# Row factors of a graph-attention layer fetched from DRAM by SyncE, and the first expert gathers placed later

## The chip, the cores and the metric

The kernel runs on one core of one Trainium2 chip. The metric is device time in microseconds (us) of one execution. Engines are named as in the profile: PE is TensorE (PEld its weight loads), DVE is VectorE, ACT is ScalarE, POOL is GpSimd, SP is SyncE. SP computes nothing here; it issues transfers. POOL issues the gathers and scatters whose rows are given by a list of indices. A queue name such as SPq or POOLq is the instruction stream of that engine.

## The reference, cut to what matters

The input is a matrix x of 3327 rows and 256 columns and a symmetric 0/1 adjacency matrix of 3327 by 3327. Two layers follow each other, each with two residual steps:

```
x = x + L0_gnn(layernorm(x), adj)        # attention over the graph, 2 heads of 128 columns
x = x + L0_ffn(layernorm(x))             # 16 experts, 2 of them for each row
x = x + L1_gnn(layernorm(x), adj)        # attention over the graph, 1 head of 256 columns, elu
x = x + L1_ffn(layernorm(x))             # 30 steps of a recurrence with a 256x256 product
```

The attention of layer 0, for row i, column j and head h:

```
s1, s2 = per row and head, two numbers          # products of the row with fixed vectors
e   = leaky_relu(s1[i] + s2[j], 0.2)
att = softmax over j of e, only where adj[i, j] == 1
out[i] = sum_j att[i, j] * W3h[j]
```

Because the exponential of a leaky relu is the larger of two exponentials, the kernel never computes a 3327 by 3327 exponential. It keeps one factor per row i (`row`) and two or three per column j (`full`, `part`, `minus`), and each weight is `relu(row_i * full_j - part_j) + part_j`, multiplied by the adjacency bit. The softmax's sum comes out of the same product, from a column of ones that stands beside W3h.

The expert step of layer 0 takes for every row the two experts with the largest gate values, and adds the two results with their weights.

## The kernel before, in words

**Tiling.** The rows are in 26 tiles of 128 (NT, the last tile has 127 rows). The attention of a layer is the function `attend` (L201). It works in parts: a part is one group of row tiles and one head. In layer 0 the groups (L45) have 4, 6, 6, 6 and 4 tiles, and each is done for head 0 and then head 1, so there are ten parts; in this text they are numbered 0 to 9. In layer 1 there is one head and the groups have three tiles (the last one has two), which gives nine parts.

**One part.** For each of the 26 column tiles j, three engines take turns. ACT makes `e`, 128 by n*128 numbers, from the row factors `rb` (L276). DVE adds and masks with the adjacency into `pT` (L281). PE multiplies each of the n tiles of `pT` with the features of tile j and accumulates into PSUM (L286); each of these float32 products is two PE instructions. `e` and `pT` have three buffers each. When a part is through, `close` (L252) divides by the sums, and after head 1 it goes on to the group's routing. This is done in small steps during the columns of the next part (L291).

**Row factors.** `rb` holds the row factors of the part's rows, the same on all 128 partitions. There are two such buffers (`rows_p`, L506). In layer 0, `row_factors` (L229) makes them on chip: for every tile of the part PE multiplies the factor column, repeated, with the identity matrix (L243, again two PE instructions for each tile), and ACT copies the result from PSUM into `rb` (L247), at most four tiles in a copy. In layer 1 only the first part does that. There, `put_factors` (L221) turns all factors with one PE transposition, DVE copies them to SBUF, and SP writes them to a DRAM tensor `factors`; the later parts are filled by one SP transfer each that reads the same DRAM rows for all 128 partitions (L234).

**Order.** The code calls `row_factors` for the following part at the middle column of the running part (L273, j = 13). What is executed is set by the framework's planner: it keeps the data dependences, takes the code's order as the priority, and puts an instruction ahead of others on its engine when it expects it to be ready first. A buffer of a pool is given to whoever comes first in that order once it is free. The trace shows such moves: the L243 products of parts 0, 1 and 2 all run from 48.74 us on, before the first attention product. [...]

**The graph.** The adjacency arrives in five pieces, one per group of row tiles (`take_graph`, L310). POOL issues the load of a piece into one DRAM buffer (`in_bytes`), and SP issues transposing transfers from there into SBUF (L335). The pieces of groups 0 to 2 are requested ahead of the attention; those of groups 3 and 4 by the last list scatter of groups 0 and 1 (L605). As there is one `in_bytes`, each piece waits for the transpositions of the one before.

**Routing.** `route` (L510) is a generator. For a finished group it normalizes the rows (DVE, one power on POOL at L120, table written by ACT's queue), turns them (L147), computes the gate products (L526), picks two experts (DVE) and finds each row's place in its expert's list. It then hands out list scatters, two for each tile, issued by POOL (L592), through the queue `later`. Behind those of group 2 comes `begin_tiles` (L890): `find_tiles` reads the lists back over SP (L663) and computes which rows the first 16 expert slots take (`which`), then three gathers are issued (L894), then the weights of slot 0 (L897).

**Experts.** A slot is 128 rows for one expert; there are at least 61. POOL gathers the rows (L757), PE turns them (L822) and multiplies (L831, L847), and POOL scatters the results (L851). SP loads the weights, three matrices of 512 KB for a slot; there are three sets of buffers. The first set, `first_set`, has its own space, the other two lie where the attention's features were, so their loads wait until the attention's last product. A gather writes into a tile of the pool `rows_p`, three slots to a tile: the first gathers use the same two buffers as `rb`.

The recurrence at the end (from L1014) is not touched.

Of the kernel before, what the change touches and what calls it, by code (L numbers as in the profile page):

```python
# [11 lines left out]
F32 = mybir.dt.float32  # L12
# [8 lines left out]
P = 128  # L21
# [9 lines left out]
def gat_moe_gat_recurrent_ffn(ctx: ExitStack, tc: tile.TileContext, a: dict, out: bass.AP):  # L31
    nc = tc.nc
    N, D = a["x"].shape
    KD = D // P
    NT = (N + P - 1) // P
# [9 lines left out]
    groups0 = [range(0, 4), range(4, 10), range(10, 16), range(16, 22), range(22, 26)]  # L45
# [152 lines left out]

    quick = []

    def attend(sc, wh, heads, row_groups, per_bank, finish, finished, pools, later, leave=False, spread=None):  # L201

        work, rows_p, ps_r, ps_o = pools
        W = wh.shape[3]
        most = max(len(ts) for ts in row_groups)
        parts = [(ts, h) for ts in row_groups for h in range(heads)]

        if spread:
            queue, room = spread
            factors = dram.tile([NT * heads, P], F32, name=f"factors{heads}")

        def put_factors():  # L221

            p = ps_r.tile([P, 512], F32, name="bank")[: NT * heads, :P]
            nc.tensor.transpose(p, sc.row.rearrange("p t h -> p (t h)"), ident)
            lines = room()[: NT * heads, :P]
            nc.vector.tensor_copy(lines, p)
            queue.dma_start(factors, lines)

        def row_factors(ts, h):  # L229

            rb = rows_p.tile([P, most * P], F32, name="rb")
            if spread and (ts, h) != parts[0]:
                here = factors[ts[0] * heads + h : ts[0] * heads + h + 1, :]
                queue.dma_start(  # L234
                    rb[:, : len(ts) * P].rearrange("p (c q) -> p c q", q=P),
                    bass.AP(tensor=here.tensor, offset=here.offset, ap=[[0, P], [heads * P, len(ts)], [1, P]]),
                )
                return rb
            for c0 in range(0, len(ts), 4):
                some = ts[c0 : c0 + 4]  # L240
                p = ps_r.tile([P, 4, P], F32, name="bank")
                for c, t in enumerate(some):
                    nc.tensor.matmul(  # L243
                        p[:, c, :], lhsT=sc.row[:, t, h : h + 1].to_broadcast([P, P]), rhs=ident,
                        start=True, stop=True,
                    )
                nc.scalar.copy(  # L247
                    rb[:, c0 * P : (c0 + len(some)) * P], p[:, : len(some), :].rearrange("p c q -> p (c q)")
                )
            return rb  # L250

        def close(ts, h, po):  # L252

            for c, t in enumerate(ts):
                pr = rows(t)
                r = small.tile([P, 1], F32, name="r")
                nc.vector.reciprocal(r[:pr], po[c][:pr, W - 1 : W])
                finish(t, pr, h, po[c][:pr, : W - 1], r[:pr])
                yield
            if h == heads - 1:  # L260
                yield from finished(ts)

        closing = iter(())
        following = row_factors(*parts[0])
        for k, (ts, h) in enumerate(parts):
            n = len(ts)
            rb = following
            acc = [ps_o.tile([P, 512], F32, name=f"acc{q}") for q in range((n + per_bank - 1) // per_bank)]
            po = [acc[c // per_bank][:, (c % per_bank) * W : (c % per_bank + 1) * W] for c in range(n)]
            for j in range(NT):  # L270
                if spread and j == 2 and k == 0:
                    put_factors()
                if j == NT // 2 and k + 1 < len(parts):  # L273
                    following = row_factors(*parts[k + 1])
                e = work.tile([P, most * P], F32, name="e")
                nc.scalar.activation(  # L276
                    e[:, : n * P], rb[:, : n * P], AF.Relu,
                    scale=sc.full[:, j, h : h + 1], bias=sc.minus[:, j, h : h + 1],
                )
                pT = work.tile([P, most * P], F32, name="pT")  # L280
                masked = nc.vector.scalar_tensor_tensor(  # L281
                    pT[:, : n * P], e[:, : n * P], sc.part[:, j, h : h + 1],
                    adjT[:, j // 2, ts[0] * P : (ts[-1] + 1) * P, j % 2], op0=ALU.add, op1=ALU.mult,
                )
                for c in range(n):
                    nc.tensor.matmul(  # L286
                        po[c], lhsT=pT[:, c * P : (c + 1) * P], rhs=wh[:, j, h, :],
                        start=(j == 0 and c % per_bank == 0), stop=(j == NT - 1),
                        skip_group_check=True,
                    )  # L290
                if j >= 2 and (next(closing, later) is later and later and later[0] in quick or later and j % 2 == 0):  # L291
                    later.popleft()(masked.ins)
            for _ in closing:
                pass
            while later and later[0] in quick:
                later.popleft()(None)
            closing = close(ts, h, po)
        if leave:
            return closing
        for _ in closing:  # L300
            pass
        while later:
            later.popleft()(None)
# [42 lines left out]
    dram = ctx.enter_context(tc.tile_pool(name="dram", bufs=1, space=bass.MemoryType.DRAM))  # L346
# [35 lines left out]
    with ExitStack() as moe:  # L382
# [16 lines left out]
        H = 2  # L399
        C = D // H  # L400
        keep = moe.enter_context(tc.tile_pool(name="keep0", bufs=1))
        wh = keep.tile([P, NT, H, C + 1], F32, name="wh")
        sc = Scores(keep, H)
        ps = moe.enter_context(tc.tile_pool(name="ps0", bufs=4, space=PSUM))
        ps_o = moe.enter_context(tc.tile_pool(name="ps0o", bufs=2, space=PSUM))
# [99 lines left out]
        run = moe.enter_context(tc.tile_pool(name="edge0", bufs=3))  # L505
        rows_p = moe.enter_context(tc.tile_pool(name="rows0", bufs=2))  # L506
# [3 lines left out]
        def route(ts):  # L510
# [97 lines left out]
            for j, t in enumerate(ts):  # L608
                for s in range(2):
                    later.append(partial(list_tokens, j, t, s))  # L610
            if ts is groups0[2]:
                pieces = begin_tiles()

                def piece(behind):
                    if next(pieces, pieces) is not pieces:
                        later.appendleft(piece)

                quick.append(piece)
                later.append(piece)
# [18 lines left out]
        first_set = hold.tile([P, 3 * KD * HID], F32, name="first_set")  # L638
# [114 lines left out]
        def gathered(s):  # L753
            if s % 3 == 0 or s == ALWAYS:
                places.append(rows_p.tile([P, MOST * P], F32, name="rb"))
            row = places[-1][:, (s % 3) * D : (s % 3 + 1) * D]
            nc.gpsimd.indirect_dma_start(  # L757
                out=row, out_offset=None, in_=table_x[: EARLY * P, :] if s < FIRST else table_x,
                in_offset=bass.IndirectOffsetOnAxis(ap=which[:, s : s + 1], axis=0),
            )  # L760
            return row
# [78 lines left out]
        ahead = deque()  # L840
# [49 lines left out]
        def begin_tiles():  # L890

            yield from find_tiles(EARLY, 0, FIRST)
            yield
            for s in range(3):  # L894
                ahead.append(gathered(s))
            yield
            weights(0)  # L897

        later = deque()
        closing = attend(sc, wh, H, groups0, 3, add_scaled, route, (run, rows_p, ps, ps_o), later, True)  # L900
        ahead.append(gathered(3))
        weights(1)

# [37 lines left out]
    ps = ctx.enter_context(tc.tile_pool(name="ps2", bufs=2, space=PSUM))  # L941
    with ExitStack() as st:
# [3 lines left out]
        wh = s_wh[:, :, :, 2:]  # L946
        sc = Scores(keep, 1, s_wh[:, :, 0, 0:2].rearrange("p t (s h) -> p t s h", h=1))
        work = st.enter_context(tc.tile_pool(name="work2", bufs=2))
        ps_o = st.enter_context(tc.tile_pool(name="ps2o", bufs=2, space=PSUM))
# [37 lines left out]
        run = st.enter_context(tc.tile_pool(name="edge2", bufs=3))  # L987
        rows_p = st.enter_context(tc.tile_pool(name="rows2", bufs=2))
        fin = st.enter_context(tc.tile_pool(name="fin2", bufs=2))
# [11 lines left out]
        def begin_state(ts):  # L1001
# [5 lines left out]

        attend(
            sc, wh, 1, groups2, 1, add_elu, begin_state, (run, rows_p, ps, ps_o), deque(),
            spread=(nc.sync, lambda: fin.tile([P, D], F32, name="low")),  # L1010
        )


    with ExitStack() as st:  # L1014
        ps_t = st.enter_context(tc.tile_pool(name="ps3t", bufs=2, space=PSUM))
        turns = cycle((ps, ps_t))
        ps_o = st.enter_context(tc.tile_pool(name="ps3o", bufs=2, space=PSUM))
# [62 lines left out]
        parts = [(step, ts) for step in range(N_STEPS) for ts in groups]  # L1080
# [53 lines left out]
```

## Time and profile before

| | us |
|---|---|
| median of three runs (1946.14 to 1951.07) | 1948.44 |
| the profiled execution, its own time | 1946.91 |
| its span | 1945.2 |
| first attention product of layer 0 | at 52.19 |
| last attention product of layer 0 | about 391.3 |
| expert slots | 391 to 745 |
| attention of layer 1 | 791 to 1090 |
| recurrence | 1094 to the end |

Times "at" are from the start of the span. In layer 0 a part with six tiles has 26 columns of 12 product instructions, one with four tiles 26 columns of 8. Busy times of PE are modelled, so where it matters the reading goes by counts and by the time between rows. The group rows of the page give the number of instructions, their busy time and mean; the chain of waits follows the work that ended last back to what released it.

### The profile page before, as it was taken

The page shows a single profiled execution, that of the slowest core. Times are in us where ns is not written, and L with a number is a line of the kernel's source. Part 1 is how long each engine was busy: PE and PEld are TensorE (multiplying, and loading weights), DVE is VectorE, ACT ScalarE, POOL GpSimd, SP SyncE. Part 2 cuts the span into 40 slices and gives each one's busy share as a digit, 9 for nine tenths or more (in the row PEclk, how much of TensorE's full clock was granted, in tenths as well). Part 3 has the DMA queues.
Part 4 walks back from the last instruction along what each step waited for, and adds up shares of the span by engine and source line. Part 5 has one row for each costly group of instructions (what it writes and reads, how often), then busy time and mean ns, then how long its engine had stood idle before and what let it go on. Part 6 is the DMA issues. An engine that isn't in the chain of part 4 may idle for free.

```text
span 1945.2 us, 33722 instructions
## 1 busy us (share of the span) xinstructions
PE 1899.3 (98%) x11987; PEld 1745.9 (90%) x11987; DVE 1278.6 (66%) x3828; ACT 1100.8 (57%) x1593; POOL 938.9 (48%) x864
## 2 busy tenths in 40 slices
PE   7999999989999998999999999999999999999998
PEld 6999999989999996888888888888888888888887
DVE  6888788832222225477766777777777777777777
ACT  2977766721111112666655666666666666666664
POOL 3010202354333331001000488888888888888886
PEclk9999999999999998999999999999999999999999
DMA  8978051089999875000000100000000000000003
GB/s 170 120 104 116 10 86 51 18 295 292 350 336 335 290 249 174 9 21 13 18 20 11 36 1 1 1 1 1 1 1 1 1 1 2 1 1 1 1 1 119
DMA packets 140946, 158.61 MB, mean 82 GB/s; under 512 B 52168, under 2 KB 100555, under 8 KB 140777
## 3 DMA queue, kind: packets, MB, share of 16 engines
q1 hardware_dynamic: 124657, 123.57, 20.5%
q0 software_dynamic: 11440, 28.09, 8.4%
q10 hardware_dynamic: 4680, 4.76, 0.7%
q8 instruction: 98, 1.61, 0.3%
q14 instruction: 71, 0.58, 0.1%
HBM read 166.09 MB, written 29.80 MB: 101 GB/s over the span
## 4 chain that ended last, share of the span: by engine, by line
PE 72%; issue 9%; DVE 5%; POOL 5%; DMA 2%; ACT 0%; another core or an unknown queue 0%; SPq 0%; POOLq 0%; DVEq 0%; ACTq 0%
PE po L1063 35%; PE acc L286 23%; PE bank L1048 9%; POOL given L851 2%; DVE pT L281 2%; PE bank L831 2%; POOL rb L757 2%; DMA given<-wh,to 2%; PE acc L847 1%; PE acc L162 1%; PE bank L526 1%; POOL rstd L120 0%; PE bank L147 0%; DVE x L961 0%
## 5 line engine op out<-in xcount | busy, mean ns | idle before, releaser
L1063 PE MATMUL po<-wc,zT 128*128 128x256 f32 x3120 | 692.9, 380 | 0.0
L1063 PEld LDWEIGHTS po<-wc,zT 128*128 128x128 f32 x3120 | 585.3, 190 | 75.5
L1039 POOL TENSOR_TENSOR th<-th,x 128x1024 f32<-128x1024 f32 (+1 forms) x210 | 460.9, 2217 | 101.9 <-ACT th L1037 100.3
L276 ACT ACTIVATE e<-rb,minus,full 128x384 f32<-128x384 f32 (+3 forms) x494 | 400.4, 824 | 179.3 <-DVE pT L281 161.0
L281 DVE SCALAR_TENSOR_TENSOR pT<-e,part,adjT 128x384 f32<-128x384 f32 (+3 forms) x494 | 380.4, 774 | 131.9 <-PE acc L286 112.4
L1045 DVE BATCH_NORM_STATS2 stats<-z 128x6 f32<-128x256 f32 x780 | 273.9, 413 | 147.6 <-ACT z L1040 147.6
L1069 DVE SCALAR_TENSOR_TENSOR x<-po,rr,bb 128x256 f32<-128x256 f32 x780 | 321.0, 474 | 59.3 <-PE po L1063 57.5
L1058 ACT COPY zT<-bank 128x512 f32<-128x512 f32 x390 | 200.9, 599 | 270.2 <-PE bank L1048 270.2
L286 PE MATMUL acc<-wh,pT 128*128 128x129 f32 x2704 | 309.5, 276 | 1.6 <-DVE pT L281 1.6
L286 PEld LDWEIGHTS acc<-wh,pT 128*128 128x128 f32 x2704 | 305.0, 192 | 2.1 <-DVE pT L281 2.0
L286 PE MATMUL acc<-s_wh,pT 128*128 128x257 f32 x1352 | 296.1, 382 | 2.7 <-DVE pT L281 2.7
L286 PEld LDWEIGHTS acc<-s_wh,pT 128*128 128x128 f32 x1352 | 257.7, 191 | 40.9 <-DVE pT L281 4.8
L120 POOL TENSOR_TENSOR rstd<-ve,neg_half 128x4 f32<-128x4 f32 (+3 forms) x28 | 31.0, 1109 | 392.5 <-DVE ve L118 307.4
L1028 POOL TENSOR_TENSOR rr<-rr,neg_half 128x4 f32<-128x4 f32 (+1 forms) x210 | 209.2, 996 | 17.5
L1040 ACT ACTIVATE z<-th 128x1024 f32<-128x1024 f32 (+1 forms) x210 | 200.9, 1019 | 1.3 <-POOL th L1039 1.3
L1037 ACT ACTIVATE th<-x 128x1024 f32<-128x1024 f32 (+1 forms) x210 | 199.2, 1010 | 1.7 <-DVE x L127 1.7
L1048 PE MATMUL bank<-ident,z 128*128 128x128 f32 x1560 | 187.7, 273 | 1.6 <-DVE high L996 1.6
L1048 PEld LDWEIGHTS bank<-ident,z 128*128 128x128 f32 x1560 | 177.0, 141 | 12.4 <-ACT zT L1058 1.8
L881 DVE TENSOR_TENSOR pT<-e,bank 128x512 f32<-128x512 f32 x61 | 41.9, 687 | 183.2 <-PE bank L831 123.1
L831 PEld LDWEIGHTS bank<-hT,wh 128*128 128x128 f32 x1280 | 150.7, 194 | 8.3 <-ACT hT L823 6.4
L831 PE MATMUL bank<-hT,wh 128*128 128x128 f32 x1280 | 151.9, 278 | 5.8 <-ACT hT L823 5.8
L877 ACT ACTIVATE e<-bank 128x512 f32<-128x512 f32 x61 | 36.4, 597 | 189.6 <-issue 85.5
(192 smaller groups left out, 1331.7 us busy)
## 6 DMA issues: line engine op xcount, KB each, us to landing
wh<-in_w_dram SPq DMA_DIRECT2D x120, 512.0 KB
first_set<-in_w_dram SPq DMA_DIRECT2D x63, 512.0 KB
in_bytes<-in_adj_dram POOLq DMA_DIRECT2D x3, 2496.0 KB
x<-in_x_dram SPq DMA_DIRECT2D x6, 512.0 KB
kept<-x SPq DMA_DIRECT2D x8, 384.0 KB
old<-kept SPq DMA_DIRECT2D x6, 512.0 KB
out_dram<-x SPq DMA_DIRECT2D x6, 512.0 KB
table_x<-row ACTq DMA_DIRECT2D x3, 768.0 KB
```

The lines of the kernel that those rows point to most:

```text
L276: nc.scalar.activation(e[:, : n * P], rb[:, : n * P], AF.Relu, scale=sc.full[:, j, h : h + 1], bias=sc.minus[:, j, h : h + 1],)
L281: masked = nc.vector.scalar_tensor_tensor(pT[:, : n * P], e[:, : n * P], sc.part[:, j, h : h + 1], adjT[:, j // 2, ts[0] * P : (ts[-1] + 1 ...
L286: nc.tensor.matmul(po[c], lhsT=pT[:, c * P : (c + 1) * P], rhs=wh[:, j, h, :], start=(j == 0 and c % per_bank == 0), stop=(j == NT - 1), s ...
L831: nc.tensor.matmul(p[:, f, :], lhsT=w[:, k, f * P : (f + 1) * P], rhs=hT[:, k, :], start=(k == 0), stop=(k == KD - 1),)
L1028: nc.gpsimd.tensor_tensor(r[:, :n], r[:, :n], neg_half[:, :n], ALU.pow)
L1039: nc.gpsimd.tensor_tensor(th[:, :n, :], th[:, :n, :], hs, ALU.add)
L1040: nc.scalar.activation(z[:, :n, :], th[:, :n, :], AF.Silu, scale=1.0 / S)
L1045: nc.vector.bn_stats(stats[:, j, :], z[:, j, :])
L1048: nc.tensor.transpose(pt[j // 2][:, j % 2, k, :], z[:, j, k * P : (k + 1) * P], ident)
L1058: nc.scalar.copy(zT[:, 2 * c : 2 * c + 2, :, :], pt[c])
L1063: nc.tensor.matmul(po[:, j, :], lhsT=zT[:, j, k, :], rhs=wc[:, k, :], start=(k == 0), stop=(k == KD - 1),)
L1069: nc.vector.scalar_tensor_tensor(x[:, ts[0] + j, :], po[:, j, :], rr[:, j : j + 1], bb, op0=ALU.mult, op1=ALU.add)
```

## The change

`attend` now always takes a triple: the queue for the transfers, the number `by_dma` of the first part whose row factors come by transfer, and a function that gives SBUF room for the turned factors. In layer 1 the triple has the same queue, 1 and the same room as before. In layer 0 it is SP's queue, 4 and the buffer `first_set`. So layer 0 also writes its factors to a DRAM tensor (52 rows of 128 numbers), in column 2 of part 0; parts 0 to 3 make `rb` by products and copies as before, and parts 4 to 9 fill it by one SP transfer each, 128 partitions by six or four runs of 512 bytes.

The code now asks for a part that comes by transfer at column 4 of the part before; the others stay at column 13. This also moves layer 1's requests from column 13 to column 4.

The three first gathers leave `begin_tiles`. They are now issued at the end of the routing of group 3, just after its list scatters have been handed to `later`. The steps of `begin_tiles` are otherwise the same, with one less between the end of `find_tiles` and the weights of slot 0.

```diff
-    def attend(sc, wh, heads, row_groups, per_bank, finish, finished, pools, later, leave=False, spread=None):
+    def attend(sc, wh, heads, row_groups, per_bank, finish, finished, pools, later, spread, leave=False):
...
-        if spread:
-            queue, room = spread
-            factors = dram.tile([NT * heads, P], F32, name=f"factors{heads}")
+        queue, by_dma, room = spread
+        factors = dram.tile([NT * heads, P], F32, name=f"factors{heads}")
...
             rb = rows_p.tile([P, most * P], F32, name="rb")
-            if spread and (ts, h) != parts[0]:
+            if parts.index((ts, h)) >= by_dma:
...
-                if spread and j == 2 and k == 0:
+                if j == 2 and k == 0:
                     put_factors()
-                if j == NT // 2 and k + 1 < len(parts):
+                if j == (4 if k + 1 >= by_dma else NT // 2) and k + 1 < len(parts):
                     following = row_factors(*parts[k + 1])
...
             for j, t in enumerate(ts):
                 for s in range(2):
                     later.append(partial(list_tokens, j, t, s))
+            if ts is groups0[3]:
+
+                for s in range(3):
+                    ahead.append(gathered(s))
             if ts is groups0[2]:
                 pieces = begin_tiles()
...
             yield from find_tiles(EARLY, 0, FIRST)
             yield
-            for s in range(3):
-                ahead.append(gathered(s))
-            yield
             weights(0)
...
-        closing = attend(sc, wh, H, groups0, 3, add_scaled, route, (run, rows_p, ps, ps_o), later, True)
+        closing = attend(
+            sc, wh, H, groups0, 3, add_scaled, route, (run, rows_p, ps, ps_o), later,
+            (nc.sync, 4, lambda: first_set), True,
+        )
...
-            spread=(nc.sync, lambda: fin.tile([P, D], F32, name="low")),
+            (nc.sync, 1, lambda: fin.tile([P, D], F32, name="low")),
```

## The prediction, made before the changed kernel was run

> **What bounds the kernel now.** First the page: how busy PE is, and whether anywhere it isn't.
>
> ```profile
> PE 1899.3 (98%) x11987; PEld 1745.9 (90%) x11987; DVE 1278.6 (66%) x3828; ACT 1100.8 (57%) x1593; POOL 938.9 (48%) x864
> PE   7999999989999998999999999999999999999998
> ```
>
> PE looks full, but its ends are modelled, so I check on the chain of waits between 195 and 475 us whether its instructions stand back to back where the change works (start, duration, what):
>
> ```profile
> 208.50 26.60 PE acc L286 x238
> 235.10 1.34 PE bank L243 x12
> 236.44 16.09 PE acc L286 x144
> ...
> 286.95 26.60 PE acc L286 x238
> 313.55 0.89 PE bank L243 x8
> 314.45 6.70 PE acc L286 x60
> ```
>
> 208.50 + 26.60 is 235.10, and 235.10 + 1.34 is 236.44: no gap. One instruction takes 0.112 us, a product's two 0.224, a six-tile column 1.34, a four-tile column 0.89. The L243 products are the row factors, and they stand in this row. Then the busy times of each engine by part (PE, PEld, DVE, ACT, POOL; parts 5 and 8):
>
> ```profile
> 217.50:252.50 35.00, 35.00 (x316) 35.00 (x315) 27.32 (x37) 26.53 (x28) 9.70 (x10) 1.00 0.33 30
> 331.00:367.00 36.00, 33.36 (x291) 32.65 (x291) 28.44 (x83) 23.38 (x32) 4.86 (x4) 1.00 0.23 77
> ```
>
> Part 5 is PE from end to end. In part 8, where group 3 is routed and the lists are read, PE lacks 2.6 us. Over all of 52.2 to 391.3 PE is busy 333.9 of 339.1 us.
>
> Last, the streams that the change queues its work on, first SP's (start, first to last, what), then POOL's around the gathers:
>
> ```profile
> 36.01 152.03 SPq L335 DMA_TRANSPOSE adjT<-in_bytes  x22
> 188.15 0.63 SPq L322 DMA_DIRECT2D in_bytes<-no_row  x1
> 260.68 7.47 SPq L335 DMA_TRANSPOSE adjT<-in_bytes  x4
> 319.41 0.35 SPq L663 DMA_DIRECT2D row<-lists  x1
> 330.80 0.42 SPq L796 DMA_DIRECT2D first_set<-in_w_dram  x1
> ...
> 391.46 0.37 SPq L796 DMA_DIRECT2D wh<-in_w_dram  x1
> ```
>
> ```profile
> 337.56 0.94 POOL L757 DMA_INDIRECT rb<-table_x,which  x1 [0.30 <-issue]
> ...
> 372.45 1.61 POOL L592 DMA_INDIRECT lists<-pair,ati  x1 [24.77 <-DVE x L503]
> ...
> 391.12 0.96 POOL L592 DMA_INDIRECT lists<-pair,ati  x1 [0.30 <-issue]
> 392.38 0.98 POOL L757 DMA_INDIRECT rb<-table_x,which  x1 [0.30 <-issue]
> ```
>
> SP is nearly empty, but waits long: for the group 4 graph from 188.8 to 260.7, and at 391.46 for the attention's last product, which frees the two other weight sets. POOL idles from 347.7 to 372.45 and is then packed to 396.
>
> Layer 1 already does what layer 0 is to do, so it prices the transfer:
>
> ```profile
> 792.08 0.39 SPq L227 DMA_DIRECT2D factors<-low  x1
> 793.45 29.43 SPq L234 DMA_DIRECT2D rb<-factors  x2
> 793.00:796.00 3.00, 2.90 (x7) 2.31 (x8) 1.32 (x4) 2.38 (x4) 0.00 (x0) 0.56 0.19 66
> ```
>
> The write of the factors is complete 1.4 us after its issue. The 192 KB read leaves 66 GB/s in the three microseconds (198 KB), and the next four move nothing: it lands within 2.6 us. And the second read starts when part 0 frees its buffer, not at column 13: the planner issues these as soon as they are possible.
>
> [...]
>
> **The change part by part**, against the profiled execution (span 1945.2, time 1946.91; the median shown is 1948.44, 1.5 above).
>
> *Removed from PE.* Row factors of parts 4 to 9. They run at 156.5, 196.9, 234.9, 275.3 (12 instructions each) and 313.4, 352.5 (8 each). 4 x 1.34 + 2 x 0.89 = 7.14 us. Three lie in rows of PE without a gap (156.5, 234.9, 313.4; 1.34 + 1.34 + 0.89 = 3.57). The others lie between the gate products of a routing. There the DVE chain that picks experts starts when the last gate product is done, and the L243 rows stand in front of it (1.12 of the 1.34 at 197.0), so I count these 3.57 too.
>
> *Removed from ACT.* Ten copies of 0.37 to 0.58 us. ACT has 1.03 busy of 1.34 us per column and three buffers ahead of PE: nothing. If ACT were the limit it would be some 5 us more.
>
> *Added.* One PE transposition, two instructions, about 0.22 us; one DVE copy of 52 x 128, under 0.3 us, in part 0 where DVE has 21.3 busy of 24.8; SP's write. Then six transfers on SP, 0.32 us of issue each; six-tile ones carry 393 KB, twice layer 1's, so 5 us from the row above, and up to 13 where a graph load runs beside them (at 250 to 255 the 16 engines are 1.03 busy). What hides them is the part before: each buffer is free when that part begins. Part starts, from the first `e` on ACT, are near 137, 173, 214, 251, 293, 327 and 364. Each transfer has 34 us or more, and so ends 20 us early. Uncovered, 5 us each, 30 in all.
>
> *SP's order.* Part 4's transfer can go at 137; group 3's graph is not requested before 147. Part 5's goes at 173, or behind six transpositions at 188; needed at 214. Part 6's can go at 214; group 4's graph load starts at 240.15. Part 7's at 251, or at 268 behind the graph; needed at 293. Part 8's at 293; the list read waits to 319. Part 9's at 327, or at 332.5 behind slot 0's weights; needed near 357. So no stall: 0.
>
> *The gathers.* Part 9's transfer takes the buffer of part 7, the gathers that of part 8. That is free when ACT ends part 8 (363 before, 357 after). POOL is idle then; three gathers take 3 x 1.27 = 3.8 us, and group 3's list scatters, which stand behind them, start with their indices (372.2 before, some 6.3 earlier after): done in time. The rows are needed at slot 0's first turn, at 373.2 before: it waits for part 8's last `close`, at 372.4, not for a gather. Cost 0[...]. Slot 0's weights go out one step sooner, but wait for the table at 330: 0.
>
> *Layer 1.* Requests at column 4 for 13: they already go when the buffer is free. 0.
>
> *What is late next.* The experts. They are PE-bound, 5.52 us a slot, and their weight loads start at the attention's last product, so they move with it; their stall for weights (3.65 us at 434.1) is counted from the same start and moves too. From there all of the rest follows.
>
> Sum: -7.14 + 0.22 = -6.9 us. The profiled execution would take 1940.0, the median 1941.5.
>
> **The rivals.**
>
> A, the forecast: 1941.5, own range 1938.5 to 1944.5.
>
> B, holes: the row factors at 196.9, 275.3 and 352.5 fill time in which PE would wait for ACT's copies of the turned rows. For it: gaps of 1.45 and 1.18 us in part 8. Against: the chain runs through those rows. Gain 3.57 - 0.22 = 3.35: 1945.1.
>
> C, gathers last: POOL is given the twelve scatters first. They end at 392.1, some 6.3 earlier after: 385.8. The first gather then ends at 387[...] while attention ends at 384.4.[...] Against: the buffer is free nine microseconds before the indices are.
>
> D, slower: a transfer stuck on SP. If part 6's stands behind the transpositions of group 4, it goes at 268.2 and lands at 273, 23 us after part 5 is through: -6.9 + 23, some 1964. It decides at SP's order alone: behind the wait that begins at 188.8 it costs this, before it nothing. Against: its buffer is free at 214, before that graph is even requested. Transfers with later needs lose nothing.
>
> E, the experts' start: SP and POOL streams stand otherwise against each other from 384 on, weights come late once more, and PE's clock falls as it does behind the stall of before (0.84 and 0.82 from 435 to 445). Once more 3.65 of stall and 1.9 of slow clock: 1947, between 1942 and 1952.
>
> That the change doesn't do what it says would be part 4 to 9 with L243 rows left; I see no way to that.
>
> **How the numbers follow.** A 0.58, B 0.13, C 0.07, D 0.12, E 0.10. Three runs lie 4.9 us apart, so 0.3% (5.8 us, 1942.6) is about what can be told. A lies 1.1 us beyond it, with some 2 us of its own spread: 0.7 of its chance is faster. Faster 0.43, within 0.3% 0.39 (the rest of A, B, C, half of E), slower 0.18. The range takes in A from 1938, B, C and most of E: 1938 to 1950. Gain and loss hold it together, so A's own range stands above.
>
> **What would show it.** L243 rows with 40 instructions after 48 us, not 104, counted for parts 0 to 3; six L234 rows before 391; ACT's first `e` of parts 4 to 9 without a wait for a transfer (A) or with one of many microseconds in part 6 (D). The last attention product at 384.4 (A), 387.9 (B). Gathers at about 357, ahead of the scatters (A), or at 386 (C). The first expert product a few tenths after the attention; slots still 5.52 us apart; PE's wait near 428 no longer than 3.65 us (E). I am wrong if the attention ends before 382 or after 388, or if its gain is not there at 745.

## The result, and the profile after

The changed kernel takes 1941.62 us (median of 9 runs, 1940.24 to 1945.2), the kernel before beside it 1948.91 (9 runs, 1946.14 to 1951.07). The ratio is 0.9968, 95% interval 0.9959 to 0.9976: 7.3 us less. The profiled execution has a span of 1938.7 us, against 1945.2.

The page of the changed kernel, PE's busy time and its 40 slices:

```profile
PE 1891.4 (98%) x11924; PEld 1736.0 (90%) x11924; DVE 1278.7 (66%) x3829; ACT 1097.0 (57%) x1583; POOL 939.8 (48%) x864
PE   7999999989999997999999999999999999999998
```

By the page PE is busy for 7.9 us less, at the same share of the span. The groups by line, up to 392 us, show the products of row factors before, then those that are left after the change, and the turn of all factors that is new:

```profile
L243 PE MATMUL bank<-ident,row 128*128 128x128 f32 x104 | 13.4, 277 | 0.0
```

```profile
L242 PE MATMUL bank<-ident,row 128*128 128x128 f32 x40 | 5.2, 276 | 0.0
...
L223 PE MATMUL bank<-ident,row 128*52 128x128 f32 x1 | 0.3, 295 | 0.1
```

There are 40 instructions where there were 104. In the chain of waits the two stretches of products that an L243 row cut in two before (at 235.10 and 313.55) are now one row each:

```profile
210.90 38.90 PE acc L285 x346
...
287.14 29.59 PE acc L285 x262
```

The two windows shown of before, in parts 5 and 8 (PE, PEld, DVE, ACT, POOL, then clock, DMA share, GB/s):

```profile
217.50:252.50 35.00, 35.00 (x314) 34.92 (x313) 28.26 (x39) 26.37 (x27) 11.26 (x12) 1.00 0.40 37
331.00:367.00 36.00, 32.76 (x283) 31.65 (x282) 30.44 (x93) 25.34 (x34) 5.33 (x4) 1.00 0.15 47
```

Part 5 is full as before. In the second window PE now lacks 3.2 us, against 2.6; the same work now comes about 4 us earlier, so the two windows do not hold quite the same products. PE's instructions show where it waits (in brackets the idle time ahead of a row and who ended it), first before, then after:

```profile
345.05 2.05 PE L286 MATMUL acc<-wh,pT 128*128 128x129 f32 x16 [1.45 <-DVE pT L281]
348.28 0.41 PE L147 MATMUL bank<-ident,row 128*128 128x128 f32 x2 [1.18 <-DVE row L127]
...
355.79 10.80 PE L286 MATMUL acc<-wh,pT 128*128 128x129 f32 x94
```

```profile
340.59 2.05 PE L285 MATMUL acc<-wh,pT 128*128 128x129 f32 x16 [1.41 <-DVE pT L280]
343.72 0.44 PE L147 MATMUL bank<-ident,row 128*128 128x128 f32 x2 [1.08 <-DVE row L127]
...
352.42 9.65 PE L285 MATMUL acc<-wh,pT 128*128 128x129 f32 x84 [0.69 <-DVE pT L280]
```

The first two waits were there before. The third is new: before, part 9's row factors (eight instructions at 352.52) kept PE busy shortly ahead of this place. SP's stream after the change:

```profile
132.91 0.50 SPq L226 DMA_DIRECT2D factors<-first_set  x1
138.13 0.40 SPq L233 DMA_DIRECT2D rb<-factors  x1
176.39 12.75 SPq L334 DMA_TRANSPOSE adjT<-in_bytes  x6
189.26 0.64 SPq L321 DMA_DIRECT2D in_bytes<-no_row  x1
190.01 19.89 SPq L233 DMA_DIRECT2D rb<-factors  x2
258.20 7.58 SPq L334 DMA_TRANSPOSE adjT<-in_bytes  x4
265.88 20.26 SPq L233 DMA_DIRECT2D rb<-factors  x2
316.22 0.34 SPq L666 DMA_DIRECT2D row<-lists  x1
321.95 0.37 SPq L233 DMA_DIRECT2D rb<-factors  x1
```

The write of the factors stands behind sixteen transpositions; part 4's transfer then waits until part 2 leaves its buffer, that is, until part 3 begins. Parts 5 and 6 go between 190.0 and 209.9, ahead of the wait for group 4's graph. Part 5's has the least time, from 190 to about 213. No `e` of parts 4 to 9 waits for a transfer. POOL's stream:

```profile
359.29 1.04 POOL L760 DMA_INDIRECT rb<-table_x,which  x1 [16.07 <-ACT d L583]
...
362.06 1.44 POOL L760 DMA_INDIRECT rb<-table_x,which  x1 [0.30 <-issue]
367.96 1.58 POOL L591 DMA_INDIRECT lists<-pair,ati  x1 [4.46 <-DVE x L502]
```

The gathers went ahead of the scatters.

**A measure for the stage.** The time from the span's start to this stage varies: the same kernel had it at 111.16 in one execution and at 114.30 in another. So the stage is measured from PE's first turned row of group 0 (L147, 111.16 before, 112.00 after) to its first expert product (391.27 and 386.79). The expectations call this R. All removed products lie in it and the added turn, at 50.6, does not, so the prediction's sum says that R falls by 7.14. The *tail* is the rest of the span. As windows, first of before, then of after:

```profile
111.16:391.27 280.11, 275.09 (x2432) 272.36 (x2433) 229.81 (x484) 199.87 (x224) 61.05 (x53) 1.00 0.38 61
```

```profile
112.00:386.79 274.79, 269.32 (x2369) 265.74 (x2369) 229.11 (x484) 195.51 (x214) 61.92 (x53) 1.00 0.42 71
```

Exactly 64 weight loads are gone (2433 to 2369), and 6.62 us of load time. But the time without a load has grown, from 280.11 - 272.36 = 7.75 to 274.79 - 265.74 = 9.05 us. So R fell by 5.32, not 7.14. The other 1.2 us of the span's 6.5 came from elsewhere: 2.0 less in the tail, 0.8 lost ahead of R.

R can be cut at instructions that every kernel here has: PE's first turned row of group 1, that of group 2, and the first product on the lists. Before:

```profile
190.80 0.67 PE L147 MATMUL bank<-ident,row 128*128 128x128 f32 x4 [0.65 <-DVE row L127]
...
269.26 0.67 PE L147 MATMUL bank<-ident,row 128*128 128x128 f32 x4 [0.66 <-DVE row L127]
...
321.08 0.20 PE L667 MATMUL bank<-ones,seen 128*16 128x1 f32 x2
```

And after:

```profile
190.30 0.76 PE L147 MATMUL bank<-ident,row 128*128 128x128 f32 x4 [0.56 <-DVE row L127]
...
266.43 0.76 PE L147 MATMUL bank<-ident,row 128*128 128x128 f32 x4 [0.56 <-DVE row L127]
...
316.66 0.20 PE L670 MATMUL bank<-ones,seen 128*16 128x1 f32 x2
```

| stretch of R | row factors of part | removed | before | after | gain |
|---|---|---|---|---|---|
| 1 | 4 | 1.34 | 79.64 | 78.30 | 1.34 |
| 2 | 5 and 6 | 2.68 | 78.46 | 76.13 | 2.33 |
| 3 | 7 and 8 | 2.23 | 51.82 | 50.23 | 1.59 |
| 4 | 9 | 0.89 | 70.19 | 70.13 | 0.06 |

Part 4's products are given back in full, part 9's not at all. A second execution of the kernel before repeats its four stretches to 0.03 us, a second one of the changed kernel to 0.30.

### The profile page after: what moved, and what is told of

Same layout as the page of the kernel before. It is cut to its first block, busy times and chain, and to the rows that moved or that the text cites. A ratio compares the mean times of both kernels' runs of the same rounds, so it can differ in the third digit from the quotient of the medians.

```text
span 1938.7 us, 33598 instructions
## 1 busy us (share of the span) xinstructions
PE 1891.4 (98%) x11924; PEld 1736.0 (90%) x11924; DVE 1278.7 (66%) x3829; ACT 1097.0 (57%) x1583; POOL 939.8 (48%) x864
## 3 DMA queue, kind: packets, MB, share of 16 engines
q8 instruction: 97, 1.59, 0.3%
## 4 chain that ended last, share of the span: by engine, by line
PE 72%; issue 9%; DVE 5%; POOL 5%; DMA 2%; ACT 1%; another core or an unknown queue 0%; POOLq 0%; SPq 0%; DVEq 0%; ACTq 0%
PE po L1066 35%; PE acc L285 23%; PE bank L1051 9%; DVE pT L280 2%; POOL given L854 2%; POOL rb L760 2%; PE bank L834 2%; DMA given<-wh,to 2%; PE acc L162 1%; PE acc L850 1%; PE bank L147 1%; PE bank L525 1%; POOL rstd L120 0%; DVE st L115 0%
```

## The experiments

Two theories stood against each other for the 1.8 missing microseconds: the rows between the gate products (those of parts 5, 7 and 9) filled holes, which is the prediction's rival B, or removing any product brings the next limit nearer. Then: which part of the change counts, is SP's order the risk that rival D saw, and what belongs to the tail?

**Transfers without the gathers.** The three gathers go back into `begin_tiles`:

```diff
-            if ts is groups0[3]:
-                for s in range(3):
-                    ahead.append(gathered(s))
...
+            yield
+            for s in range(3):
+                ahead.append(gathered(s))
```

> The changed kernel with the three first gathers put back behind the tables of the first slots. On SP, part 9's transfer then stands behind the weights of slot 0. Stretch R is from PE's first turned row of group 0 to PE's first expert product: 280.1 us before, 274.8 in the changed kernel. Theory (the moved gathers keep part 9's buffer free): the gathers take the buffer that part 7 leaves, part 9's transfer waits for part 8's last row-factor read, lands 3 to 5 us later, PE stands about 5 us at the start of part 9, R 279 to 281, total within 0.15% of before. Rival (the place of the gathers is worth nothing): R 274 to 276, total as the changed kernel, ratio 0.9965.

Measured: 1937.0 us, ratio 0.9959 (0.9944 to 0.9973), R 275.73. The trace of this kernel, SP's and ACT's rows near part 9's start:

```profile
359.34 0.37 SPq L233 DMA_DIRECT2D rb<-factors  x1
...
362.91 5.41 ACT L275 ACTIVATE e<-rb,minus,full 128x512 f32<-128x512 f32 x7 [3.49 <-DVE seen L565]
```

As the buffers are shared, part 9's transfer now waits for part 8's buffer and goes 37 us later, and ACT stands still for 3.5 us. The profile names a DVE step there, but the bytes arrive until about 362.4 (69, 156 and 61 GB/s in the three microseconds from 360), and the changed kernel, with the same DVE step, has no such wait. So the mechanism that was expected is there, but R is not at 279 to 281. Stretches 1 to 3 are those of the changed kernel's second execution to 0.01 us; stretch 4 is 71.60, for 70.13 and 70.12. The gathers' new place protects part 9's transfer, and that is worth 1.5 us of R, not 5: PE itself waited only 0.91 us for the late `pT`. In the total it can't be told.

**The gathers alone.** The kernel before, with only the gathers moved.

> The kernel before with only the gathers moved, all row factors by products. Theory: R 280.1 within 0.5, total within 0.1% of before, because the gathers were not on the path before. Rival (a part of the gain is the gathers'): R under 279.

Measured: 1946.73, ratio 1.0006 (0.9998 to 1.0014), R 281.42. The gain is the transfers'. But R is not within 0.5 of before: it is 1.31 longer, all of it in stretch 4 (71.50 for 70.19). PE has two waits there that the kernel before does not have:

```profile
358.71 8.08 PE L286 MATMUL acc<-wh,pT 128*128 128x129 f32 x70 [0.38 <-DVE pT L281]
...
393.80 3.84 PE L835 MATMUL bank<-hT,first_set 128*128 128x128 f32 x32 [0.46 <-ACT hT L827]
```

With the gathers moved, ACT can copy part 9's row factors as soon as their products are through, in the middle of group 3's routing, at 354.76 (353.70 + 1.06); in the kernel before, where the gathers had taken that buffer, the copy came at 363.56, behind part 8's last `e`. When the copy went and what it alone costs was not shown. Together with the run above: moving the gathers costs 1.3 us of R when part 9's factors are products, leaving them costs 1.5 when these come by transfer, and both steps together cost nothing (70.13).

**The products twice.** The kernel before, where each L243 product of parts 4 to 9 is done twice, with the same result:

```diff
+                    for _ in range(2 if parts.index((ts, h)) >= 4 else 1):
                         nc.tensor.matmul(
...
```

> The kernel before with the row-factor products of parts 4 to 9 done twice, 64 PE instructions more, nothing else. Theory of the prediction (each such product costs its PE time wherever it stands): R 280.1 + 7.1 = 287.2, ratio 1.0037. Rival (those of parts 5, 7 and 9 stand in the routing, where something else sets the pace): R 283.7 to 286.

Measured: 1950.18, ratio 1.0028 (1.0017 to 1.0039), R 287.03: 6.92 more, of 7.14 added. The trace has 168 of these instructions where there were 104. So PE pays for these products nearly in full, in rows with and without gaps. Removing them gives back less.

**The changed kernel again.**

> The changed kernel as it is, once more. R is 274.8 as in its first profile if R is set by the order of instructions. From the first expert product to the end of the span the first profile has 1551.9 us, against 1553.9 before. Theory: these 2.0 us come from the TensorE clock granted after waits (0.53 and 1.00 against 0.65 and 0.57 around 745 to 797 us) and change from run to run, so the tail here differs from 1551.9 by a microsecond or more. Rival: the tail is 1551.9 within 0.3, a property of the order.

Measured: 1938.19, ratio 0.9959 (0.9947 to 0.9972). R 274.27, 5.84 below before; load time 265.38, so 8.89 us without a load. The missing 1.3 to 1.8 us is no accident of one execution. R itself moved by 0.52. The tail is 1550.42, where the first execution had 1551.91: as the theory said, it changes from run to run by more than a microsecond; that the clock does it is not shown.

**Half of the parts by transfer.** Odd: parts 5, 7, 9, whose products stood between gate products. Even: parts 4, 6, 8, whose products stood in rows without a gap.

```diff
+        def by(k):
+            return k >= by_dma and (heads == 1 or k in (5, 7, 9))     # (4, 6, 8)
...
-            if parts.index((ts, h)) >= by_dma:
+            if by(parts.index((ts, h))):
...
```

> The changed kernel with transfers for parts 5, 7 and 9 alone; parts 4, 6 and 8 by products again. In the kernel before, the row factors of 5, 7 and 9 stand between the gate products of a routing. Stretch R (from PE's first turned row of group 0 to its first expert product; 280.1 us before, 274.8 and 274.3 in the changed kernel). Theory now (in the routing the next limit, DVE's chain, stands close behind PE, so taking PE work away there gains only a part): R 278.0 to 278.9, a gain of 1.2 to 2.1. Rival, the prediction's sum: a gain of 3.6, R 276.5.

> The changed kernel with transfers for parts 4, 6 and 8 alone; parts 5, 7 and 9 by products again. These row factors stood in gapless rows of attention products. Theory and the prediction's sum agree here: a gain of 3.4 to 3.6, R 276.5 to 276.8. Rival (gains in the changed kernel are spread evenly over the six parts): a gain of 2.7, R 277.4.

Measured, odd: 1947.12, ratio 0.9994 (0.9986 to 1.0003), R 278.61, 1.50 less. Even: 1946.23, ratio 0.9993 (0.9984 to 1.0002), R 277.85, 2.26 less. Each half holds 3.57 us of products. By stretches, the change against the kernel before, with the products removed in brackets:

| stretch of R | 1 | 2 | 3 | 4 |
|---|---|---|---|---|
| odd parts | +0.10 (0) | -0.97 (1.34) | -0.63 (1.34) | 0.00 (0.89) |
| even parts | -1.35 (1.34) | -1.34 (1.34) | -0.81 (0.89) | +1.24 (0) |

The even parts, whose products stood in rows without a gap, give back 3.50 of 3.57. What they lose is in stretch 4, where nothing was removed: it is the loss of the run with the gathers alone, for here too part 9's factors are products beside moved gathers. So R missed its expectation for a reason that is not in it. The odd parts, whose products stood between gate products, give back 1.60 of 3.57, as the theory for that run said: less than the prediction's 3.57 and more than rival B's 0. So it is not true that the removal of any product loses a part: the loss belongs to the routing. PE's row of the odd kernel in part 8:

```profile
356.84 9.65 PE L289 MATMUL acc<-wh,pT 128*128 128x129 f32 x84 [0.69 <-DVE pT L284]
```

The 0.69 us hole comes with part 9's removed products, worth 0.89: at this one place rival B was right. Without the even kernel's stretch 4 the two halves give 5.0, the changed kernel 5.3 and 5.8: its own two executions lie as far apart as that difference, so no help of one half to the other can be told from it.

**All parts by transfer.** `by_dma` 1 for 4, on SP's queue, and once on ACT's.

```diff
-            (nc.sync, 4, lambda: first_set), True,
+            (nc.sync, 1, lambda: first_set), True,     # and (nc.scalar, 1, ...)
```

> The changed kernel with transfers for all parts but the first. In SP's stream the write of the factors and part 1's transfer then stand behind the sixteen transpositions of the first three graph pieces, as the write already does in the changed kernel, where it goes at 132.9 us. Theory (an instruction on SP waits for all before it): part 1, due at 77 us, starts only near 135 to 140, about 55 to 65 us late, total near 1995 to 2005. Rival (the transfers are asked for early and the write finds its way between the pieces): total 1934 to 1940.

Measured on SP: 2007.54 us (one run), span 2005.8, just above the range of the theory. SP's stream and ACT's first `e` of part 1:

```profile
36.59 92.71 SPq L334 DMA_TRANSPOSE adjT<-in_bytes  x16
129.39 0.50 SPq L226 DMA_DIRECT2D factors<-first_set  x1
132.45 0.94 SPq L233 DMA_DIRECT2D rb<-factors  x2
```

```profile
136.27 4.34 ACT L275 ACTIVATE e<-rb,minus,full 128x512 f32<-128x512 f32 x6 [62.54 <-DMA rb<-factors]
```

Rival D's mechanism is real: the write stands behind the first sixteen transpositions, and an early part loses 62 us. `by_dma` = 4 is what keeps the change clear of it, with part 4's transfer out at 138.13.

> As the kernel with transfers for all parts but the first, but issued by ACT's queue, where no graph transfer stands. Theory (what holds parts 1 to 3 is SP's stream alone): the products of parts 1 to 3 are saved too, 0.9 + 1.3 + 1.3 us at most, against a start that waits about 2 us for the write of the factors on ACT, and nine issues of 0.4 us on an engine with slack: total 1 to 4 us under the changed kernel, ratio to before 0.994 to 0.9960. Rival (ACT's waits for its own transfers cost more than the products): total above the changed kernel's.

Measured on ACT's queue: 1993.26, ratio 1.0235 (1.0221 to 1.0249). The expectation failed. The 2 us for the write were the author's estimate; in layer 1 the read goes 1.37 us after it (792.08 to 793.45). ACT's stream:

```profile
86.97 0.30 ACTq L226 DMA_DIRECT2D factors<-first_set  x1
87.65 2.22 ACT L275 ACTIVATE e<-rb,minus,full 128x512 f32<-128x512 f32 x3 [34.93 <-DMA factors<-first_set]
...
124.40 0.39 ACTq L233 DMA_DIRECT2D rb<-factors  x1
124.89 4.34 ACT L275 ACTIVATE e<-rb,minus,full 128x512 f32<-128x512 f32 x6 [14.83 <-DMA adjT<-in_bytes]
```

ACT itself stands still for 34.9 us at the write and for 14.8 us at part 2's transfer. Behind the second wait the trace names a transposition that SP issued, and SP's stream is full of them there:

```profile
36.13 96.51 SPq L334 DMA_TRANSPOSE adjT<-in_bytes  x15
```

Part 2's transfer reads nothing of the graph. At the first wait the trace names only the write itself, which went at 86.97; what held it until then is not shown. The two queues are two instruction streams, but here ACT's waited for SP's work.

**Four buffers of turned rows.** Do the holes in the routing come because PE runs out of `pT`? In the changed kernel and in the one before, `pT` gets a fourth buffer in layer 0 and in the experts (of the edit only the line of layer 0 is shown).

```diff
-                pT = work.tile([P, most * P], F32, name="pT")
+                pT = work.tile([P, most * P], F32, name="pT", bufs=4 if heads == 2 else 3)
```

> The changed kernel with the turned rows pT in four buffers instead of three in layer 0 and in the experts. R is the time from PE's first turned row of group 0 to PE's first expert product: 280.1 before, 274.8 and 274.3 changed, where the removed products come to 7.14 less 0.22, so 1.1 to 1.6 us are missing. Theory (PE runs out of turned rows while a routing holds DVE and ACT, a backlog of one more row carries it over): R 272.9 to 273.7, the 0.69 us wait for pT in part 8 gone. Rival (DVE's or the routing's own total time sets the end there, a backlog only moves the wait): R 274.2 to 274.9, the wait stays or appears a part later. Total time: theory 0.5 to 1.5 us below the changed kernel, rival the same.

> The kernel before with the same four buffers. Theory: with the L243 products still in place PE is the limit nearly everywhere, R falls by 0 to 0.6 from 280.1, so 279.5 to 280.1, and the time is that of the kernel before within 0.1 per cent. Rival: the same holes exist before, hidden in no product, and R falls as much as in the changed kernel, to 278.7 or less.

Measured, changed: 1942.04, ratio to before 0.9994 (0.9986 to 1.0002), R 274.12. Before: 1944.56, ratio 1.0009 (1.0001 to 1.0016), R 279.06. PE's rows of the first:

```profile
338.05 2.05 PE L285 MATMUL acc<-wh,pT 128*128 128x129 f32 x16 [0.70 <-DVE pT L280]
...
349.88 11.29 PE L285 MATMUL acc<-wh,pT 128*128 128x129 f32 x84 [0.69 <-DVE pT L280]
```

And its windows there:

```profile
350.00:352.00 2.00, 2.00 (x11) 2.00 (x12) 2.00 (x5) 1.97 (x3) 0.00 (x0) 0.56 0.00 0
352.00:354.00 2.00, 2.00 (x13) 2.00 (x13) 1.79 (x5) 1.95 (x3) 0.00 (x0) 0.59 0.00 0
354.00:356.00 2.00, 2.00 (x21) 2.00 (x20) 1.85 (x5) 1.45 (x2) 0.00 (x0) 1.00 0.00 0
```

The wait of 1.41 us is halved, but the 0.69 stays, and after it PE ran for four microseconds at a clock of 0.56 to 0.59: the 84 products took 11.29 us, where the changed kernel took 9.65 after the same wait. These 1.64 us of slow clock hide what the buffer gave; R lands just below the rival's range for another reason than the rival's. The kernel before had no such stretch, and there the buffer gave 1.01 of R, between the two expectations. So about a microsecond of holes was a matter of buffers already before the change. In the changed kernel R without the slow clock would be about 272.5 (an estimate, 274.12 - 1.64), 1.8 to 2.3 below its two executions: a part of what the change lacks may be a matter of buffers too, but no run without the slow clock shows it. And nothing of it reaches the total: by their R the two should be 6.0 and 1.0 us below the kernel before, and they are 1.8 below and 0.7 above. Where these 4 and 2 us go, one profile each (tails 1553.10 and 1550.80) doesn't show. In the first PE waits 3.63 us for a `pT` of the experts at 395.25, where the changed kernel waits 0.82 or not at all; the rest is open.

**The kernel before again.**

> The kernel before once more, for what one and the same program shows twice. Theory (the 2 us that came after the first expert product are not the change's): R 279.6 to 280.6, the tail from the first expert product to the end of the span anywhere from 1549 to 1556. Rival (the tail is the kernel's own, and the changed kernel's is 2 us shorter): R the same, tail 1553.4 to 1554.4.

Measured: 1946.68 us (one run), span 1945.0, R 280.07, tail 1550.63. R repeats to 0.04 us, the tail, 1553.93 in the first profile, does not. PE's waits among the first experts, first execution, then second:

```profile
397.57 0.94 PE L831 MATMUL bank<-hT,wh 128*128 128x128 f32 x6 [2.13 <-ACT hT L823]
437.77 5.47 PE L831 MATMUL bank<-hT,wh 128*128 128x128 f32 x32 [3.65 <-ACT hT L823]
```

```profile
399.53 0.91 PE L831 MATMUL bank<-hT,wh 128*128 128x128 f32 x6 [0.99 <-DMA wh<-in_w_dram]
...
459.56 3.81 PE L831 MATMUL bank<-hT,wh 128*128 128x128 f32 x32 [1.00 <-DMA wh<-in_w_dram]
```

One and the same program stalls for 3.65 us at 437.8 once, and not at all there the next time. The changed kernel did the same: 3.58 us at 433.2 in its first profile, none there in its second.

## Why the prediction was right, and where it was not

The time, 1941.6 against 1941.5, and the sign are right; so are most steps. One term was too large, and the total came out by the help of a term put at nothing.

*Removed from PE: -7.14.* The count is right (40 instructions left, 64 gone). The step that failed is "so I count these 3.57 too", for the products of parts 5, 7 and 9 between the gate products. Measured by stretches they give back 1.60: 0.97 of 1.34, 0.63 of 1.34 and nothing of 0.89. The other half, in rows without a gap, gives back 3.50 of 3.57. In all, the removal is worth 5.32 and 5.84 of R. The reading that these rows stand in front of DVE's chain did not make them worth their length: when they go, PE waits for DVE's turned rows instead (0.69 us in part 8), and 1.1 to 1.3 us more of time without a load come up; apart from the 0.69 it is spread over tenths. Doubling the same products costs 6.92: the full engine paid for what was added, but gave back what was removed only until its next wait. Rival B had the right places and the right kind of loss, and put it at about twice its size (3.57, measured 1.97).

*Added, ACT, layer 1.* The turn is one record of 0.3 us. Layer 1 is worth nothing by the program itself: with column 13 for 4 the changed program has the same instructions in the same order on all five engines. That ACT's copies are worth nothing was not tried alone.

*SP's order: 0.* Right for all six transfers. Predicted at 137, 188, 214, 251 or 268, 293 and 327 to 332, they went at 138.13, 190.01, by 209.9, 265.88, by 286.1 and 321.95. The 5 us of a six-tile transfer and the 13 beside a graph load were estimates: part 4's traffic fell off by 143, 5 us after its issue (111, 199 and 61 GB/s in the three microseconds from 140, then 1), part 5's beside a graph load by about 196, 6 us after (251, 205, 204, 370, 370 and 86 in the six from 190, then 16). How far a read stands behind the write of what it reads shows in the run with all parts on SP, where the buffer is free, 129.39 to 132.45: 3.06 us just behind the graph's transpositions, where layer 1 took 1.4. Rival D failed in this kernel by its own test, and the run with all parts on SP shows what it would have cost.

*The gathers: 0.* Right for this kernel: at 359.29, ahead of the scatters, with stretch 4 as before. It holds only because part 9's factors come by transfer; beside products the same move costs 1.3 us of R. What gathers behind the scatters would cost, rival C's case, was not shown, as no row here times a gather's landing; part 9's late transfer, the nearest thing to it, cost 1.5.

*The experts move along: 0.* Right in that their first product follows the attention at once, 386.79. Wrong in that the stall of 3.65 "moves too": it is no property of the program. The attention's end was predicted at 384.4; the gain there was 4.48, and 3.33 at the last slot, 741.38 before and 738.05 after. The prediction named this as a sign of being wrong, a gain that is not there at 745, and it came in part. The span's 6.5 was complete only after layer 1's attention, 1083.77 for 1090.28. For rival E there is no sign: the tail did not grow.

*The sum.* So of the 7.3 us between the medians 5.3 to 5.8 are shown to be the removed products. The other 1.5 to 2 lie outside this stage: in the profiles the tail gave 2.0 and the start lost 0.8, and the tail of two executions of the unchanged program differs by 3.3. The second comparison gave 7.2 and the kernel with transfers alone 8.4, so part of it may belong to the program; which part, no run here settles. That the total met the forecast to 0.1 us is luck to that extent.

## What to carry to other kernels

Price work that is removed from a full engine twice: by its duration, and by the slack of the next limit in that stage; doubling the work tells the first price only (6.92 us here, where the removal gave 5.32 and 5.84). To see where a gain is lost, cut the stage at instructions that all kernels share. When a change has two steps, run each alone: here either one alone costs over a microsecond of the stage that both together do not. Before a wait in one profile goes into a forecast, see it in a second execution of the same program. When a transfer is given to a busy queue, find the last moment at which it may go and what stands ahead of it (with all parts on SP 16 transpositions, 62.54 us), and look in the trace for what it waits for, not only at the queue's name (14.83 us on ACT's).

## What the runs showed that was not expected

- ACT stood still at its own transfers for 34.93 and 14.83 us. Behind the second wait the trace names a transposition issued by SP: here a second issuer waited for the first one's work.
- After the same wait of 0.69 us PE's granted clock was 1.00 in the changed kernel (352 to 356 us) and 0.56 to 0.59 in the one with four buffers (350 to 354), which cost 1.64 us. Why it fell there is not shown.
- In the experts from 442 to 600 us the DMA engines are busy 0.98 to 0.99 of the time in the eleven profiles other than the two of kernels with all parts by transfer. PE is busy 154.9 to 157.9 of these 158 us in the same eleven, so both are near full.
